# Third hop of a graph layer as seven products, with its weights applied after it

## The chip, the cores and the metric

The kernel runs on one NeuronCore of a Trainium2 chip. Its engines work side by side and meet through semaphores: TensorE (PE, with PEld its weight loads), VectorE (DVE), ScalarE (ACT), GpSimd (POOL) and SyncE (SP), which only starts transfers. The metric is the device time of one execution in microseconds (us), as the median of several runs.

## The reference

Two graph layers on 2048 nodes, 64 features and a batch of 8. Each row of `adj` has equal non-zero entries (one over the row's degree), so a product with it, a hop, is a product with a matrix S of zeros and ones, scaled by row with r.

```python
# layer 0: Chebyshev, K = 3, weights of each node from a 16-wide embedding
w = einsum('nd,dkio->nkio', embedding, weight)       # b in the same way
A_stack = [I, A, 2 A A - I]
x_g = einsum('knm,bmc->bnkc', A_stack, x)
x = layernorm(x + einsum('bnki,nkio->bno', x_g, w) + b)
# layer 1: five matrices from two supports, both adj
x_cat = concat[h, A h, 2 A A h - h, A h, 2 A A h - h]
x = layernorm(h + x_cat @ W + bias)                  # h: output of layer 0
```

With W in five blocks of 64 rows, layer 1 is h v0 + A (h v1 + A (h v2)) + bias, where v0 = I + W0 - W2 - W4, v1 = W1 + W3, v2 = 2 (W2 + W4). Two hops serve each layer: the first and second for x, the third and fourth for h.

## The kernel before

**Tiles.** Nodes are cut into 16 tiles of 128 (index t for results, k for sources). z0, z1 and z2 each hold 16 tiles of 128 x 512 values (batch times features). S is made on the chip from slabs of `adj` by a test against zero (`places`, L196) or against the row's r with a count of the equal places (`places_equal`, L201). A value is split into a high and a low half (`high` on ACT, `low` on DVE), and PE multiplies S with both, so a block costs two matmuls of 512 columns (`add_block`, L229).

**First and second hop.** `hop_x` (L396) runs over k in two passes, counts S's places (`nonzero`, ACT, L445) and writes four sums of quarters of S as bf16 into DRAM (`sums_of`). The second hop, `seven_products` (L460), takes the four quarters of S and the batch in two halves and forms seven products in place of eight blocks, a Strassen scheme: 7 products of 8 steps `kk`, 8 matmuls each (L529), with S as the moving operand, so the result comes out transposed. M1 with B11 needs quarter (0, 0) of S, M6, M7, M5 and M3 load sums, M2 and M4 load quarters. `sum_of_y` makes sums and differences of y on DVE; `put` adds a finished product to the results.

**The mix of layer 0.** `mix0` (L321) goes through 16 node tiles. For each it multiplies x, the first and the second hop, transposed, with all 16 embedding slices of the weights: eight groups of 24 float32 records on PE (L342), each group followed by four multiply-adds on DVE (L348) into `acc`, which POOL has started (L328). Then come `layernorm` (L303: sums on DVE, subtraction on POOL, squares on ACT, a root, and a multiplication on POOL, L312), a transpose of the normalized tile on PE (L268) and `project` (L353): z0 = h v2, z1 = h v1, z2 = h v0 + bias. The transpose of tile t-1 and the operands of tile t+1 are put into tile t by `between`; the projection of t-1 follows tile t.

**Third and fourth hop.** `hop_h` (L599) computes z1 += r S z0 in three passes over k, for 4, 8 and 4 result tiles, with the counting test. `hop_g` (L675) computes z2 += r S z1 for the first 8 result tiles over all k, keeping the halves of z1; `hop_tile` (L697) then does tiles 8 to 15 one by one, in two halves c of 16 matmuls, and normalizes and stores each. `check` (L648), at tile 9, compares the counts; `load_flag` (L660), at tile 10, has each engine read the flag that decides at the end whether a general program runs in addition.

**What sets the order.** A framework plans each engine's queue from a model of times. Where an instruction goes through `ordered` while `in_order` is set, or through `keep_in_program_order`, it is kept behind all that its engine has been given in program order. `run` (L236) takes a list of steps; each has parts with a lead, and a part with lead 2 is written two steps ahead of its use. `todo` holds small pieces of work, two of which are written after each step. PSUM has four tiles of two banks (`bank`, L81), given out in turn; a new tile waits until the last reader of the old one is done. SP's loads stay in program order, with five buffers for raw slabs.

Of the kernel before, what the change touches and what calls it, by code (L numbers as in the profile page):

```python
# [8 lines left out]
F32 = mybir.dt.float32  # L9
# [28 lines left out]
def pattern(  # L38
# [20 lines left out]

    nc = tc.nc  # L60
# [13 lines left out]
    rowpool = pool(hops, "frow", 1, side="right")  # L74
    hpool = pool(hops, "fhl", HL, side="right")
# [23 lines left out]
    equal = keep.tile([P, 3 * NT], F32, tag="equal", name="equal")  # L99
# [13 lines left out]
    v = const.tile([P, 3, C], F32, tag="v", name="v")  # L113
# [122 lines left out]
    def run(steps):  # L236

        got = [{} for _ in steps]
# [23 lines left out]
    def transpose(src, tag, pt=None):  # L262
# [7 lines left out]
        nc.scalar.copy(  # L270
            tt.rearrange("p j (h n) -> p h j n", h=2), pt[:, :, : B // 2 * C].rearrange("p h (j n) -> p h j n", n=C)
        )
# [5 lines left out]
    def rsqrt(ss):  # L278


        def col(name):
            return (work if ss.shape[1] == B else keep).tile(list(ss.shape), F32, tag=f"{name}{ss.shape[1]}", name=name)

        va = col("ln_v")
        nc.vector.scalar_tensor_tensor(va, ss, 1.0 / C, eps.to_broadcast(list(ss.shape)), ALU.mult, ALU.add)
        sd = col("ln_sd")
        nc.scalar.activation(sd, ss, AF.Sqrt, bias=eps, scale=1.0 / C)  # L287
        r0 = col("ln_r0")
        nc.vector.reciprocal(r0, sd)

        q = col("ln_q")
        nc.vector.scalar_tensor_tensor(q, r0, -0.5, r0, ALU.mult, ALU.mult)
        nc.vector.tensor_tensor(q, q, va, ALU.mult)
        r = col("ln_r")
        nc.vector.scalar_tensor_tensor(r, q, 1.5, r0, ALU.add, ALU.mult)
        return r

    def square_sums(src, to):
        sq = work.tile([P, B, C], F32, tag="ln_sq", name="sq")
        nc.scalar.activation(sq, src, AF.Square)  # L300
        nc.vector.tensor_reduce(to, sq, AX.X, ALU.add)

    def layernorm(src):  # L303

        s = work.tile([P, B], F32, tag="ln_s", name="s")
        nc.vector.tensor_reduce(s, src, AX.X, ALU.add)  # L306
        nc.vector.tensor_tensor(s, s, part, ALU.mult)  # L307
        xc = xcpool.tile([P, B, C], F32, tag="ln_xc", name="xc")
        nc.gpsimd.tensor_tensor(xc, src, wide(s), ALU.subtract)  # L309
        ss = work.tile([P, B], F32, tag="ln_ss", name="ss")  # L310
        square_sums(xc, ss)
        nc.gpsimd.tensor_tensor(xc, xc, wide(rsqrt(ss)), ALU.mult)  # L312
        return xc
# [7 lines left out]
    def mix0(t, tt, between):  # L321
# [4 lines left out]
        for g in range(2):  # L326
            part = acc[:, 4 * g : 4 * g + 4, :]
            nc.gpsimd.tensor_tensor(  # L328
# [3 lines left out]
            )  # L332
            for dg in range(D // DG):
                if g == 1 and dg == D // DG - 1:
                    between()
# [10 lines left out]
                for d in range(DG):  # L346
                    dd = dg * DG + d
                    nc.vector.scalar_tensor_tensor(  # L348
                        part, pm[:, :, :, d, :].rearrange("p j i c -> p (j i) c"), emb_sb[:, t, dd : dd + 1], part, ALU.mult, ALU.add
                    )  # L350
        return layernorm(acc)

    def project(t, hT, pus=None):  # L353


        for g in range(2):
            pm = bank("pu") if pus is None else pus[g]
            for i in range(2):
                for j in range(2):
                    q = slice(j * C, (j + 1) * C)  # L360
                    nc.tensor.matmul(  # L361
                        pm[:, j, i * 3 * C : (i + 1) * 3 * C], lhsT=hT[q, 2 * g + i, :], rhs=v[q],
                        start=True, stop=True,
                    )
            got = pm[:, :, : 6 * C].rearrange("p j (i k c) -> p j i k c", i=2, k=3)
            bs = slice(4 * g, 4 * g + 4)
            for s in range(2):
                nc.scalar.copy(bc(s, t)[:, bs, :].rearrange("p (i j) c -> p j i c", j=2), got[:, :, :, 2 - s, :])
            nc.vector.tensor_tensor(
                bc(2, t)[:, bs, :].rearrange("p (i j) c -> p j i c", j=2), got[:, :, :, 0, :],  # L370
                bias1.unsqueeze(1).unsqueeze(1).to_broadcast([P, 2, 2, C]), ALU.add,
            )
# [10 lines left out]
    S1, S2, S4, S3 = range(4)  # L383
    couple = []
# [11 lines left out]
    def hop_x(g, kk, j):  # L396
# [37 lines left out]
        def use(got):  # L434
# [10 lines left out]
            ordered(nc.scalar.activation(seen, s, AF.Copy, accum_out=nonzero[:, i : i + 1]))  # L445
            if last and g == 1:
# [13 lines left out]
    def seven_products(s, to, more):  # L460
# [3 lines left out]
        sums, kept = [], {}  # L464

        def sum_of_y(kk, name):
# [11 lines left out]
            if name == "T2":  # L478
# [4 lines left out]
                return add(y, add(y, quarter(2, 2), quarter(1, 2), ALU.subtract), quarter(1, 1), ALU.add)  # L483
            y = xcpool.tile([P, BC], F32, tag="ln_xc", name="y")
            if name == "T4":
# [573 lines left out]
```

## Time and profile before

| | |
|---|---|
| three runs, us | 838.54, 838.76, 840.05 (median 838.76) |
| profiled execution, us | 839.63 |
| its span, first to last instruction, us | 837.6 |
| mean granted TensorE clock | 0.994 |
| first hop, from 5.9 us | 116.6 |
| second hop, from 122.5 us | 102.8 |
| mix of layer 0, from 225.3 us | 366.7 |
| third hop, from 592.0 us | 119.7 |
| fourth hop, first 8 tiles, from 711.7 us | 58.2 |
| fourth hop, last 8 tiles, from 769.9 us | 58.5 |
| from the last matmul to the end | 9.2 |

Lengths are in us, read from the matmuls' records. A row of a group names line, engine, operation, result and operands, shapes and count, then busy time, mean duration and idle time before it. [...] what a stream of them costs is the spacing of their starts.

### The profile page before, as it was taken

How to read it: one execution, taken by the hardware profiler on the slowest of the kernel's cores; microseconds unless marked ns; L12 is line 12 of the kernel's file. 1: busy time of each engine (PE TensorE's matmuls, PEld its weight loads, DVE VectorE, ACT ScalarE, POOL GpSimd, SP SyncE). 2: the span in 40 equal slices, each digit the busy share in tenths (PEclk: the TensorE clock that was granted, in tenths of full speed). 3: DMA queues.
4: the chain of work that ended last, by engine and by line, in shares of the span. 5: the costliest groups of instructions: out<-in, count | busy, mean ns of one | idle time of the engine just before them, and what ended most of it. 6: DMA issues, size and time to landing. Idle time of an engine off the chain costs nothing.

```text
span 837.6 us, 14392 instructions
## 1 busy us (share of the span) xinstructions
PE 823.5 (98%) x5614; PEld 732.0 (87%) x5614; DVE 607.0 (72%) x1256; ACT 224.6 (27%) x427; POOL 128.8 (15%) x130
## 2 busy tenths in 40 slices
PE   9999999999999999999999999989999999999995
PEld 6888888888888999999999999989888878888884
DVE  6868657757878888888788888897867567534662
ACT  5436445772002111111111111101331132401210
POOL 0100000002731111111111111020101020102133
PEclk9999999999999999999999999999999999999998
DMA  9976775558200000000000000120256227544462
GB/s 332 394 273 221 248 258 174 154 163 289 88 14 14 11 6 13 14 14 13 14 14 13 14 14 14 42 86 2 76 182 190 94 74 240 173 142 126 132 183 92
DMA packets 57180, 96.55 MB, mean 115 GB/s; under 512 B 3984, under 2 KB 28816, under 8 KB 56976
## 3 DMA queue, kind: packets, MB, share of 16 engines
q1 hardware_dynamic: 52208, 82.69, 30.6%
q0 software_dynamic: 2304, 8.39, 3.0%
q10 hardware_dynamic: 2592, 4.47, 1.5%
q8 instruction: 47, 0.77, 0.4%
q14 instruction: 29, 0.24, 0.1%
HBM read 82.94 MB, written 12.58 MB: 114 GB/s over the span
## 4 chain that ended last, share of the span: by engine, by line
PE 93%; DVE 4%; issue 1%; DMA 0%; ACT 0%; POOL 0%; SPq 0%; DVEq 0%; POOLq 0%
PE pm L342 36%; PE acc L229 35%; PE accT L529 12%; PE a L229 7%; DVE acc L348 3%; PE pu L361 2%; PE pt L268 1%; PE first L133 1%; DVE s L205 0%; DMA raw<-in_adj 0%; POOL got L318 0%; DVE s L306 0%; ACT L287 0%; PE accT L144 0%; POOL xc L309 0%
## 5 line engine op out<-in xcount | busy, mean ns | idle before, releaser
L229 PE MATMUL acc<-hl,s 128*128 128x512 f32 x1280 | 292.7, 390 | 0.3 <-DVE acc L348 0.3
L229 PEld LDWEIGHTS acc<-hl,s 128*128 128x128 f32 x1280 | 239.4, 188 | 52.9 <-issue 1.2
L348 DVE SCALAR_TENSOR_TENSOR acc<-pm,pack_sb,acc 128x256 f32<-128x256 f32 x512 | 246.3, 483 | 43.5 <-PE pm L342 21.1
L342 PE MATMUL pm<-w,xt 64*128 64x256 f32 x1024 | 161.1, 379 | 3.1 <-DVE acc L348 2.8
L342 PE MATMUL pm<-w,z 64*128 64x256 f32 x1024 | 160.4, 378 | 0.0
L342 PE MATMUL pm<-w,t 64*128 64x256 f32 x1024 | 160.1, 377 | 0.2 <-ACT t L270 0.2
L342 PEld LDWEIGHTS pm<-w,xt 64*128 64x128 f32 x1024 | 108.1, 188 | 5.6 <-issue 1.8
L342 PEld LDWEIGHTS pm<-w,t 64*128 64x128 f32 x1024 | 110.7, 188 | 2.0 <-ACT t L270 0.6
L342 PEld LDWEIGHTS pm<-w,z 64*128 64x128 f32 x1024 | 110.8, 188 | 1.4
L198 DVE TENSOR_SCALAR s<-raw 128x1024 fp32r<-128x1024 f32 x87 | 68.1, 783 | 57.8 <-PE acc L229 48.8
L529 PE MATMUL accT<-s,hl 128*128 128x512 f32 x448 | 102.0, 389 | 0.0
L529 PEld LDWEIGHTS accT<-s,hl 128*128 128x128 f32 x448 | 84.0, 188 | 17.5
L209 ACT CAST hl<-z 128x512 fp32r<-128x512 f32 (+1 forms) x120 | 67.0, 578 | 119.1 <-PE acc L229 108.5
L213 DVE TENSOR_TENSOR hl<-z,hl 128x512 fp32r<-128x512 f32 (+1 forms) x120 | 81.5, 681 | 13.6 <-ACT hl L209 10.7
L205 DVE SCALAR_TENSOR_TENSOR s<-raw,rrow 128x512 fp32r<-128x512 f32 (+1 forms) x48 | 45.8, 956 | 26.7 <-PE acc L229 25.3
L270 ACT COPY hT<-pt 128x512 f32<-128x512 f32 x16 | 9.4, 586 | 204.4 <-PE pt L268 204.4
L309 POOL TENSOR_TENSOR xc<-acc,s 128x512 f32<-128x512 f32 x16 | 17.1, 1068 | 282.4 <-DVE s L307 282.4
L229 PE MATMUL a<-hl,s 128*128 128x512 f32 x256 | 58.5, 390 | 0.0
L229 PEld LDWEIGHTS a<-hl,s 128*128 128x128 f32 x256 | 48.0, 188 | 10.0
L258 POOL TENSOR_TENSOR z<-z,got 128x512 f32<-128x512 f32 x12 | 18.8, 1592 | 155.2 <-ACT got L257 155.1
L328 POOL TENSOR_TENSOR acc<-z,ebias 128x256 f32<-128x256 f32 x32 | 27.0, 866 | 87.1 <-ACT hl L209 85.6
L517 ACT CAST s<-raw 128x1024 fp32r<-128x1024 bf16 x32 | 33.6, 1050 | 10.6 <-ACT hl L209 10.6
(87 smaller groups left out, 477.0 us busy)
## 6 DMA issues: line engine op xcount, KB each, us to landing
raw<-in_adj SPq DMA_DIRECT2D x103, 512.0 KB, 4.5
raw<-in_adj SPq DMA_DIRECT2D x34, 256.0 KB, 3.0
sums_of<-z POOLq DMA_DIRECT2D x16, 512.0 KB, 4.9
raw<-sums_of SPq DMA_DIRECT2D x32, 256.0 KB, 2.8
xt<-in_xT SPq DMA_DIRECT2D x16, 256.0 KB, 2.7
out<-got ACTq DMA_DIRECT2D x16, 256.0 KB, 2.0
z<-in_x SPq DMA_DIRECT2D x15, 256.0 KB, 9.3
w<-in_w SPq DMA_DIRECT2D x3, 512.0 KB, 5.8
```

Of the source, the lines that this page charges most:

```text
L198: ordered(nc.vector.tensor_scalar(s, raw, 0.0, None, ALU.not_equal))
L205: ordered(nc.vector.scalar_tensor_tensor(s, raw, 0.0, r, ALU.add, ALU.is_equal, accum_out=count))
L209: ordered(nc.scalar.copy(to[0], src))
L213: ordered(nc.vector.tensor_tensor(to[1], src, to[0], ALU.subtract))
L229: nc.tensor.matmul(accs[i], lhsT=s[:, i * P : (i + 1) * P], rhs=hl[h], start=(first and h == 0), stop=(last and h == 1),)
L258: ordered(nc.gpsimd.tensor_tensor(to, to, got, ALU.add))
L309: nc.gpsimd.tensor_tensor(xc, src, wide(s), ALU.subtract)
L328: nc.gpsimd.tensor_tensor(part.rearrange("p (j i) c -> p j i c", j=2), bc(0, t)[:, 4 * g : 4 * g + 4, :].rearrange("p (i j) c -> p j i c", ...
L342: nc.tensor.matmul(pm[:, j, i], lhsT=tt[k][q, 2 * g + i, :], rhs=w[k][q, ds, :], start=(k == 0), stop=(k == 2),)
L348: nc.vector.scalar_tensor_tensor(part, pm[:, :, :, d, :].rearrange("p j i c -> p (j i) c"), emb_sb[:, t, dd : dd + 1], part, ALU.mult, ALU.add
L517: ordered(nc.scalar.copy(s, got["raw"]))
L529: nc.tensor.matmul(acc[i][:, c], lhsT=hl[h][:, i * P : (i + 1) * P], rhs=S[:, c * 512 : (c + 1) * 512], start=(kk == 0 and h == 0), stop=( ...
```

## The change

**Third hop.** z0 now holds h itself. A second call of `seven_products` computes S h, transposed, into four tiles `zT` (float32). `project` multiplies with v0 and v1 only (128 columns instead of 192). The weights v2 are applied to the result: `weigh` multiplies blocks of zT with `v[:, 2]`, and `add_weighed` adds r times that to z1. Half tiles of the first eight are weighed after products M3 and M2, the other eight tiles inside the fourth hop's first part.

**Quarters and sums.** `hop_x` also writes the quarters of S of the second half of the sources to DRAM as bf16, from ACT's queue (`quarters`), and both calls of `seven_products` load them for M2 and M4. T4's sum of y is made in place at product 3. `wait` is the number of empty pieces ahead of a product's puts: 4 in the second hop, 2 in the third.

**Order.** The layernorm of tile t is given out in four parts and kept in order with the projection of t-1. For the last tile the whole mix is kept in order, the first two steps of the third hop are written into it (`early`), and its layernorm's rest goes into `todo`. Its transpose and projection sit in product 0.

**Fourth hop.** The counting test moves there: `hop_g` serves 6 tiles instead of 8 with it, `hop_tile` does tiles 6 to 15 with it. The check comes at tile 14, the flag's matmul and its reading between the halves of tile 15.

**Memory.** rowpool and hpool stay to the end, v moves to `keep`, `equal` and `sums` change their sizes.

```diff
-    v = const.tile([P, 3, C], F32, tag="v", name="v")
+    v = keep.tile([P, 3, C], F32, tag="v", name="v")
-    equal = keep.tile([P, 3 * NT], F32, tag="equal", name="equal")
+    equal = keep.tile([P, 5 * NT], F32, tag="equal", name="equal")
...
     def hop_x(g, kk, j):
...
+            if j == 1:
+                ordered(nc.scalar.dma_start(out=quarters[kk, :, :, g, :], in_=seen))
...
     def layernorm(src, to):
...
-        nc.gpsimd.tensor_tensor(xc, src, wide(s), ALU.subtract)
+        ordered(nc.gpsimd.tensor_tensor(xc, src, wide(s), ALU.subtract))
+        yield
+        sq = squares(xc)
+        yield
...
+        ordered(nc.vector.tensor_reduce(ss, sq, AX.X, ALU.add))
+        root = rsqrt_parts(ss)
+        next(root)
+        yield
+        xc, r = (a.rearrange("p (g m) c -> p g m c", g=2) for a in (xc, wide(next(root))))
+        ordered(nc.gpsimd.tensor_tensor(to, xc, r, ALU.mult))
+        yield
...
     def mix0(t, tt, at):
...
-            nc.gpsimd.tensor_tensor(
+            ordered(nc.gpsimd.tensor_tensor(
                 part.rearrange("p (j i) c -> p j i c", j=2),
...
+                for work_here in at.get((g, dg), ()):
+                    work_here()
...
     def project(t, hT, pus=None):
...
-                        pm[:, j, i * 3 * C : (i + 1) * 3 * C], lhsT=hT[q, 2 * g + i, :], rhs=v[q],
+                        pm[:, j, i * 2 * C : (i + 1) * 2 * C], lhsT=hT[q, 2 * g + i, :], rhs=v[q, 0:2, :],
...
-    def seven_products(s, to, more):
+    def seven_products(s, to, sums, more, wait=4):
...
             def load_sum(got):
-                if isinstance(which, tuple):
+                if which == (0, 0):
                     return
...
+                if isinstance(which, tuple):
+                    load(nc.sync, raw, quarters[kk, :, which[0]])
...
+                if p == 3:
+                    sum_of_y(kk, "T4")
...
+                while p == 6 and todo:
+                    todo.pop(0)()
...
+    def weigh(ts, pairs, bs):
+        for n, t in enumerate(ts):
+            to = columns(pairs, n, bs)
+            for i in range(2 * len(bs)):
+                for j in range(2):
+                    q, block = slice(j * C, (j + 1) * C), 2 * bs[0] + i
+                    nc.tensor.matmul(
+                        to[:, j, i * C : (i + 1) * C], lhsT=zT[t // 8, t // 4 % 2][q, t % 4, block * P : (block + 1) * P],
+                        rhs=v[q, 2, :], start=True, stop=True,
+                    )
+    def add_weighed(ts, n, pairs, bs):
...
+            nc.vector.scalar_tensor_tensor(
+                to, columns(pairs, n, bs), rcol[:, t : t + 1], to, ALU.mult, ALU.add
...
+    third = seven_products(0, to_zT, sums3, {
+        (0, 4): [last_transposed],
+        (0, 6): [last_projected],
+        4: half_weighed(1, 0), 5: half_weighed(0, 1),
+    }, wait=2)
...
+        at = {(1, 3): [between]}
+        if t == NT - 1:
+
+            in_order.append(True)
+            at = {
+                (0, 1): [lambda: early(0)], (0, 3): [lambda: early(1)], (1, 0): [between],
+                (1, 1): [lambda: project(t - 1, done["hT"])],
+            }
+        norm = mix0(t, tt, at)
+        in_order.append(True)
+        next(norm)
+        if t == NT - 1:
+            todo.extend(lambda: next(norm) for _ in range(3))
+            break
...
-    EARLY = 8
+    G = 6
-    sums = keep.tile([P, 8, B], F32, tag="sums", name="sums")
+    sums = keep.tile([P, G, B], F32, tag="sums", name="sums")
...
     def hop_g(k):
...
-            got["s"] = places(slab(k, 0, HALF))
+            got["s"] = places_equal(slab(k, 0, G * P), 0, equal[:, k : k + 1])
...
+            add_block(accs[:4], s, hl, k == 0, end)
+            waiting.append((s[:, 4 * P :], hl, k == 0, end))
+            if k > 0:
+
+                while waiting:
+                    add_block(accs[4:], *waiting.pop(0))
+            if k in (1, 2, 4, 5):
+
+                ts, pairs = {1: [8, 9], 2: [10, 11], 4: [12, 13], 5: [14, 15]}[k], [sums3[0][1]]
+                weigh(ts, pairs, [0, 1])
+                for n in range(2):
+                    add_weighed(ts, n, pairs, [0, 1])
...
     def hop_tile(t, c):
...
-            got["s"] = places(raw)
+            nc.vector.scalar_tensor_tensor(
+                s, raw, 0.0, rrow[:, t * P : (t + 1) * P].unsqueeze(1).to_broadcast([P, 8, P]),
+                ALU.add, ALU.is_equal, accum_out=equal[:, i : i + 1],
+            )
...
+                if t == NT - 1:
+                    make_flag(*late_values["bad"])
+                    late_values["odd"] = load_flag()
                 return
-            if t == 9:
-                check()
-            if t == 10:
-                late_values["odd"] = load_flag()
+            if t == NT - 2:
+                late_values["bad"] = check()
```

## The prediction

> **What bounds the kernel now.** I read the page first: who is busy, and what the chain that ended last consists of.
>
> ```profile
> PE 823.5 (98%) x5614; PEld 732.0 (87%) x5614; DVE 607.0 (72%) x1256; ACT 224.6 (27%) x427; POOL 128.8 (15%) x130
> ...
> PE 93%; DVE 4%; issue 1%; DMA 0%; ACT 0%; POOL 0%; SPq 0%; DVEq 0%; POOLq 0%
> ```
>
> TensorE is the bound nearly everywhere, so a matmul removed is worth its spacing, and the 4% in which DVE carries the chain are places where TensorE was made to wait. Next the busy time by stage (columns: stretch, length, then busy time of PE, PEld, DVE, ACT, POOL, granted clock, DMA share, GB/s): layer 0 mix, third hop, fourth hop's first half, fourth hop's tiles.
>
> ```profile
> 225.30:592.00 366.70, 363.32 (x3561) 356.44 (x3560) 299.86 (x674) 52.83 (x124) 64.62 (x67) 1.00 0.06 18
> 592.00:711.70 119.70, 119.40 (x538) 97.43 (x537) 81.91 (x157) 35.20 (x62) 12.24 (x8) 1.00 0.48 149
> 711.70:769.90 58.20, 58.20 (x257) 47.92 (x256) 24.43 (x37) 10.37 (x19) 4.47 (x3) 1.00 0.52 157
> 769.90:828.40 58.50, 58.50 (x259) 47.87 (x257) 33.60 (x85) 11.94 (x25) 21.05 (x19) 1.00 0.45 138
> ```
>
> Then the chain in order of time (start, length, what), for spacings and for the loss late in the mix.
>
> ```profile
> 130.85 94.52 PE accT L529 x416
> ...
> 338.79 18.13 PE pm L342 x168
> ...
> 563.92 4.52 PE pm L342 x24
> 568.44 1.32 PE pu L361 x16
> 569.76 18.13 PE pm L342 x168
> ```
>
> A 512-column matmul of the hops costs 94.52/416 = 0.227 us. The mix's 256-column records cost 18.13/168 = 0.108 us. Twenty-four of them took 4.52 us at 563.92 instead of 24 x 0.108 = 2.6. The next windows say why: PE idle for half a window, then the clock at half.
>
> ```profile
> 561.50:565.00 3.50, 1.71 (x24) 1.49 (x21) 3.11 (x8) 1.16 (x2) 0.00 (x0) 0.99 0.00 0
> 565.00:568.30 3.30, 3.30 (x20) 3.14 (x18) 0.88 (x2) 0.00 (x0) 0.00 (x0) 0.50 0.00 0
> ```
>
> Tile 14 of the mix lasts 27.5 us from one projection to the next (540.8 to 568.2) where its neighbours take 22.57: 4.9 us are lost, because four slabs of the third hop's tests (L205, from 543.7 to 549.4) were slipped into DVE's queue there.
>
> [...] The node bias (L144, 64 columns, four row groups, two records for each float32 matmul) agrees:
>
> ```profile
> 128.73 1.07 PE L529 MATMUL accT<-s,hl 128*128 128x512 f32 x4
> 129.73 1.12 PE L144 MATMUL accT<-bias_sb 16*128 16x64 f32 x32
> 130.78 0.73 PE L529 MATMUL accT<-s,hl 128*128 128x512 f32 x2
> ```
>
> Its 32 records are 8 rounds of four, and the single records start 112 ns apart from round to round: [...]. The visit cost 1.25 us in all (129.64, when the next L529 was due, to 130.78, plus 0.11 in the slower first pair), so 0.35 us beyond 8 x 0.112 for going in and out. [...] The trace shows it once: 1.71 us busy of 3.5 tripped it, while 2.68 of 3.4 at 264.6 did not. [...]
>
> **The change, part by part**, against the profiled span of 837.6 (its own run took 839.6, 0.9 above the median of 838.76; I carry differences to the median).
>
> 1. Third hop: 7 x 8 steps of 8 matmuls are 448 instead of 512. 64 x 0.227 = **-14.5**.
>
> 2. Projection: 128 columns instead of 192. Its 16 records are 8 rounds in 1.30 us, 0.162 each, by columns. At 128 columns the columns would take 0.108, the weight load 0.112: 8 x 0.112 = 0.90, so -0.40 per tile, 16 tiles: **-6.5**. Two of four ACT copies per tile (375 ns) go too, off the path.
>
> 3. Weights behind the hop: each tile has 8 float32 matmuls of 64 columns with a fresh 128-column load, 16 records, two row groups, 8 rounds x 0.112 = 0.90. 16 tiles are 14.3, in 6 visits (two in the third hop, four in the fourth) at 0.35: **+16.5**. Bounds: were they as quick as the transposes (64 columns, 0.25 us for 8 records), 7.9 + 2.1 = 10; with load and columns one after the other (112 + 54 ns), 21 + 2 = 23. I take 16.5 because part 2's rate and L144's agree on it. So the arithmetic of 1 to 3 is -4.5.
>
> 4. Losses that go with the old order: tile 14 (-4.9), the third hop's first two matmuls, 0.99 us apart where 0.56 was usual (-0.4), and the bank boundary at 687.7 (-0.4). **-5.7**.
>
> 5. The last mix tile in written order. Before, POOL starts tile t+1's accumulator (L328) between the two layernorm multiplications, and DVE may go on as soon as ln_r is done:
>
> ```profile
> 571.79 1.04 POOL L309 TENSOR_TENSOR xc<-acc,s 128x512 f32<-128x512 f32 x1 [19.36 <-DVE s L307]
> 575.60 1.05 POOL L312 TENSOR_TENSOR xc<-xc,ln_r 128x512 f32<-128x512 f32 x1 [2.77 <-DVE ln_r L295]
> ```
>
> Now in tile 15 the start of the accumulator is queued on POOL behind tile 14's final multiplication. Counting from PE's first matmul of tile 15: ln_r is ready at 5.7, the multiplication ends 6.9, the accumulator 7.8 (0.87), DVE's first of eight groups of four (4 x 0.52 = 2.1) starts at 8.0 instead of 5.8. Nothing else stands behind it on POOL, but DVE has nothing it may do first. Into DVE's queue come two early steps of the third hop, each a low half (0.42) and a test (0.69), 1.2 with gaps; their slabs are behind the last xT on SP, issued a tile earlier. DVE ends groups 0 to 3 at 10.1, 13.4, 15.6 and 18.9. PE's four groups (2.59 each) end at 10.4; four PSUM tiles are full, the transpose of tile 14 takes the first freed, so group 4 waits for group 1: 13.5 instead of 10.6. The projection of tile 14 then waits for group 3's tile: 19.0 instead of 16.6. 2.9 + 2.4 = **+5.3**. What is late next is the layernorm of tile 15 by as much.
>
> 6. Start of the third hop. Steps 0 and 1 are ready, so PE runs 3.6 us. Behind the last group DVE has, from PE's last mix matmul: the group until 2.3, the layernorm sums 0.85, two low halves 0.9, the test of step 2 0.7: 4.8, PE wanted it at 3.7. Step 3's operands come after the wait for the squares (5.8) at 7.1, wanted 6.7; for steps 3 to 5 the sums of y (three 0.42) raise DVE's step to 2.45 against PE's 1.82. I add 1.1 + 0.5 + 0.3 + 0.8 = **+2.7**; 0 to 5 as bounds. Later products fit: DVE's fullest (T1 sums, T4 sums, low halves, four puts of 0.68) is 13 of 14.5 us; ACT's (1.05 + 0.40) x 8 is 11.6.
>
> 7. Flag. PE reads it half a tile (16 x 0.227 = 3.6 us) before its end instead of when it had long been there:
>
> ```profile
> L661 PEldq TENSOR_LOAD <-flag x1: 487/487/487, 788.0 to 788.0; - x1
> ```
>
> DVE finishes the previous layernorm 3.6 us after its tile (824.7 against 821.1), so it is free just then. The flag takes 0.13, the load 0.49, three hand-overs and a restart about 0.4: **+1.0** in which the 16 last matmuls are queued behind the load, and for them waits the tail. The other engines' loads are behind finished work; the six early tiles' stores (1.1 us of POOL, 0.35 of ACT) are over by tile 12. Bounds 0.6 and 2.5.
>
> 8. At nothing. The 16 writes of quarters (4.2 MB, ACT's queue, 0.35 us issue each) lie beside hop one, where ACT is half idle and slabs land early from step 4 on (14.4 against 20.8 at PE); without that cover 10 us of transfer would show. Casts for two products move from DVE (0.69) to ACT (1.05), inside the 1.82 us steps. Tests of the fourth hop: DVE per slab 1.04 + 0.08 + 0.75 = 1.9 of PE's 2.7 (768 columns, between the 0.79 and 1.29 of the L205 rows), with four times 1.5 us of adding beside 2.15 us of PE weighing; per tile 6.6 to 8 of 7.28, with two half tiles of lead. Were the lead gone, 1 us per tile for three tiles. Equal addresses: the tiles ahead of S grow by 512 bytes (v 768, `equal` 128, `sums` -64, five columns of its root -320), so S stands to the y halves modulo 256 as before, and I take 0; that PE's spacing would change by 2% either way is the bound I can't exclude (9 us), and nothing points to it. The tail of 9.2 us stays.
>
> Sum: -4.5 - 5.7 + 5.3 + 2.7 + 1.0 = -1.2, without the clock. The new stalls are 2.9, 2.4, then 1.1 + 0.5 and 1.0 us, each in or near a 3.4 us window. A half-clock window costs up to 1.7. The first is hidden by the wait for group 3; of the later three I charge two: +3.4. **+2.2: 841.0.**
>
> **Rivals.** (A) The forecast: seven products pay for their weights, and ordering gives back what it saved: 838.5 to 843.5, 0.55, of it 0.37 slower by over 0.2% (1.7 us, about what a measurement tells from no change) and 0.18 the same. (B) Faster: the written order costs half of parts 5 and 6 and no further half-clock window follows: -1.2 - 4.0 = 833.5; it decides once DVE reaches tile 15's first group by 6 us or PE's stalls stay under 2.5 us. For it: DVE's idle time at each tile's end; against it: the queue as written. 0.27, of it 0.23 faster. (C) DVE becomes the bound: in the first product, where it runs at 2.45 against 1.82 us, and in the fourth hop's tests and additions, 5 us more: 846. For it DVE's 82 of 120 us in the third hop already; against it the light products after the fifth. 0.18, of it 0.14 slower, 0.04 the same. (D) That seven products aren't shorter can't be: the second hop shows 448 at the same spacing.
>
> Faster 0.23, same 0.26, slower 0.51; likeliest A with 841.0. Leaving out a tenth on either side gives 834 to 846; A's own range is 838.5 to 843.5.
>
> **What would show it.** 448 third-hop matmuls at 0.227; projections of 0.90; weighing records 56 ns apart on average, 3.6 us for the visits of 8 half tiles; no loss in tile 14; waits of PE for L348 in tile 15 near 11 and 17 us after its start; half clock once or more between there and the second product; a PE gap of about 1 us half a tile from the end. Wrong if the weighing is loaded at the transposes' rate (-6), if tile 15 runs without a gap, or if stalls appear from the second product on.

## The result, and the profile after

The changed kernel took 839.98 us (median of 20 runs, 838.72 to 842.57), the kernel before 839.27 beside it: a ratio of 1.0012 (95% interval 1.0005 to 1.0019). Seven products instead of eight blocks, narrower projections and a repaired order come out about even. The profiled execution of the changed kernel took 839.43 us, its span 837.4, against 839.63 and 837.6; the two had mean clocks of 0.997 and 0.994, to which the part on the clock returns.

The page of the changed kernel, busy times and chain by engine:

```profile
PE 819.1 (98%) x5806; PEld 727.0 (87%) x5806; DVE 595.3 (71%) x1295; ACT 267.4 (32%) x464; POOL 111.9 (13%) x121
...
PE 84%; DVE 6%; DMA 5%; issue 2%; ACT 1%; POOL 1%; SPq 0%; ACTq 0%; DVEq 0%; POOLq 0%
```

TensorE has 4.4 us less work than before (823.5), and the chain leaves it more often: DMA carries 5% of it where it carried none, DVE 6% instead of 4%. The stages (first hop, mix, third hop, then the fourth hop's two parts; columns as before):

```profile
5.99:123.50 117.51, 117.28 (x514) 96.28 (x513) 87.68 (x139) 58.24 (x105) 8.93 (x16) 1.00 0.93 327
...
226.50:588.00 361.50, 356.75 (x3561) 348.79 (x3560) 292.66 (x665) 44.73 (x97) 60.90 (x66) 1.00 0.07 21
588.00:701.90 113.90, 112.15 (x603) 92.37 (x602) 69.71 (x162) 73.75 (x116) 2.16 (x2) 1.00 0.43 142
701.90:754.00 52.10, 52.10 (x321) 43.14 (x320) 33.42 (x61) 5.55 (x9) 0.00 (x0) 1.00 0.46 141
754.00:827.70 73.70, 72.93 (x323) 59.88 (x321) 46.98 (x118) 13.14 (x28) 24.81 (x18) 1.00 0.46 147
```

| stage, by the starts of TensorE's records, us | before | after | difference |
|---|---|---|---|
| first hop | 116.5 | 117.55 | +1.0 |
| second hop | 102.9 | 102.9 | 0 |
| mix | 366.7 | 361.6 | -5.1 |
| third hop | 119.7 | 113.8 | -5.9 |
| fourth hop, to the last matmul | 116.4 | 125.6 | +9.3 |
| from the last matmul's start | 9.5 | 9.9 | +0.4 |

The mix and the third hop give 11 us, the weighing (8.6 us) and the flag (0.8) in the fourth hop take most of it, and the first hop takes one. Below, "the changed kernel" is the profile above; times of other kernels are given as ratios to the kernel before, run beside them.

### The profile page after: what moved, and what is told of

It reads as the page before. It is cut to its first block, busy times and chain, and to the rows that moved or that the text cites. A ratio compares the mean times of both kernels' runs of the same rounds, so it can differ in the third digit from the quotient of the medians.

```text
span 837.4 us, 14780 instructions
## 1 busy us (share of the span) xinstructions
PE 819.1 (98%) x5806; PEld 727.0 (87%) x5806; DVE 595.3 (71%) x1295; ACT 267.4 (32%) x464; POOL 111.9 (13%) x121
## 4 chain that ended last, share of the span: by engine, by line
PE 84%; DVE 6%; DMA 5%; issue 2%; ACT 1%; POOL 1%; SPq 0%; ACTq 0%; DVEq 0%; POOLq 0%
PE pm L362 36%; PE accT L561 24%; PE a L231 8%; PE acc L231 7%; PE accT L231 5%; DMA quarters<-seen 4%; DVE acc L368 3%; PE accT L671 2%; PE pu L381 1%; DMA raw<-in_adj 1%; PE pt L274 1%; DMA z<-in_x 1%; DVE s L200 1%; DVE z L416 1%; ACT seen L468 1%
## 5 line engine op out<-in xcount | busy, mean ns | idle before, releaser
L561 PE MATMUL accT<-s,hl 128*128 128x512 f32 x896 | 205.6, 390 | 1.7 <-DVE s L200 1.7
L561 PEld LDWEIGHTS accT<-s,hl 128*128 128x128 f32 x896 | 167.5, 188 | 37.8 <-ACT sq L310 1.8
L231 PE MATMUL acc<-hl,s 128*128 128x512 f32 x512 | 117.5, 391 | 0.2 <-DVE z L453 0.2
L549 ACT CAST s<-raw 128x1024 fp32r<-128x1024 bf16 x96 | 100.8, 1050 | 44.3 <-ACT hl L211 32.4
L231 PEld LDWEIGHTS acc<-hl,s 128*128 128x128 f32 x512 | 96.1, 188 | 21.5 <-DVE z L453 1.4
L211 ACT CAST hl<-z 128x256 fp32r<-128x256 f32 (+1 forms) x96 | 47.5, 510 | 62.5 <-PE acc L231 27.7
L231 PE MATMUL accT<-hl,s 128*128 128x512 f32 x192 | 44.9, 392 | 0.0
L231 PEld LDWEIGHTS accT<-hl,s 128*128 128x128 f32 x192 | 35.7, 188 | 7.6
L200 DVE TENSOR_SCALAR s<-raw 128x1024 fp32r<-128x1024 f32 x47 | 33.2, 706 | 11.8 <-PE acc L231 8.0
L468 ACT ACTIVATE seen<-s 128x1024 bf16<-128x1024 f32 x32 | 33.7, 1053 | 17.9 <-DMA quarters<-seen 17.9
```

The costliest lines, as they stand in the source:

```text
L200: ordered(nc.vector.tensor_scalar(s, raw, 0.0, None, ALU.not_equal))
L211: ordered(nc.scalar.copy(to[0], src))
L231: nc.tensor.matmul(accs[i], lhsT=s[:, i * P : (i + 1) * P], rhs=hl[h], start=(first and h == 0), stop=(last and h == 1),)
L549: ordered(nc.scalar.copy(s, got["raw"]))
L561: nc.tensor.matmul(acc[i][:, c], lhsT=hl[h][:, i * P : (i + 1) * P], rhs=S[:, c * 512 : (c + 1) * 512], start=(kk == 0 and h == 0), stop=( ...
```

## The experiments

### The flag's place

```diff
                 if t == NT - 1:
                     make_flag(*late_values["bad"])
-                    late_values["odd"] = load_flag()
                 return
+            if t == NT - 1:
+                late_values["odd"] = load_flag()
```

> After the change TensorE stands still for 0.96 us half a tile from its end, while DVE makes the flag and TensorE reads it. Here the flag is made at the same place, but read only behind the last 16 matmuls. Theory (the 16 matmuls queue behind the reading): the gap falls to the 0.3 us that the flag's own small matmul costs, so about 0.65 us less than the changed kernel's 839.98, that is 839.3. Rival (the reading only moves into the tail, where DVE, ACT or POOL now read it while the last tile waits): the gap goes, the stretch after the last matmul grows by 0.5 us, and the time stays at 840.0.

Measured: 839.41 us, 1.0000 (0.9992 to 1.0008): 0.6 less than the changed kernel by the medians, 1.0 by the ratios, whose intervals overlap, so that the trace is the firmer evidence. TensorE's timeline, first of the changed kernel, then of this one (start, length, what; in brackets idle time before it and what ended it):

```profile
823.01 0.19 PE L763 MATMUL pf<-ones,bad 128*1 128x1 f32 x2
823.96 3.91 PE L231 MATMUL a<-hl,s 128*128 128x512 f32 x16 [0.77 <-DVE flag L764]
```

```profile
823.96 0.19 PE L763 MATMUL pf<-ones,bad 128*1 128x1 f32 x2
824.08 3.94 PE L231 MATMUL a<-hl,s 128*128 128x512 f32 x16
```

From the flag's matmul to the next takes 0.12 us instead of 0.96, and the stretch from the last matmul's start grows by 0.1 only (9.95 to 10.04), against the rival. The queue behind the reading was the cost: 0.84 us, more than the 0.65 of the theory.

### POOL's start set free, and the place of the early steps

The first kernel takes the start of the accumulator out of the written order; the second does that too and moves the two early steps.

```diff
-            ordered(nc.gpsimd.tensor_tensor(part..., bc(0, t)..., ebias..., ALU.add))
+            nc.gpsimd.tensor_tensor(part..., bc(0, t)..., ebias..., ALU.add)
```
```diff
-                (0, 1): [lambda: early(0)], (0, 3): [lambda: early(1)], (1, 0): [between],
-                (1, 1): [lambda: project(t - 1, done["hT"])],
+                (1, 0): [between], (1, 1): [lambda: project(t - 1, done["hT"])],
+                (1, 2): [lambda: early(0)], (1, 3): [lambda: early(1)],
```

> One edit to the changed kernel: in the last mix tile POOL's start of the accumulator is not kept behind tile 14's final multiplication. Theory (step 5: DVE's first group waits for this start): DVE begins about 2.2 us earlier, TensorE's two waits in tile 15 (2.49 and 1.39 us) shrink to under 1.5 us together, and the time falls by 2.0 to 2.5 us to about 837.7. Rival (DVE's own work in tile 15, the two early steps of 1.2 us each, sets the waits): they stay above 3 us together, and the time stays within 0.5 us of 840.0.

> As the kernel with POOL's start set free, and the two early steps of the third hop put before the last two groups of tile 15 instead of the second and the fourth. Theory (DVE is short in the whole of tile 15 and the third hop's start, where it is idle for under 1.5 us): the wait at tile 14's projection (2.27 us there for 0.89 of work) goes, and the start of the third hop, 11.68 us for its first 40 matmuls, loses as much; the time stays within 0.5 us of 838.97. Rival (only the place of the two steps made TensorE wait): both together fall by 1.4 us, and the time to 837.5.

Measured: 838.97 us, 1.0000 (0.9991 to 1.0009), and 837.76, 0.9986 (0.9980 to 0.9993). TensorE's waits in tile 15 and at the third hop's start, in the changed kernel:

```profile
575.12 0.70 PE L362 MATMUL pm<-w,xt 64*128 64x256 f32 x4 [2.30 <-DVE acc L368]
...
580.06 0.70 PE L362 MATMUL pm<-w,xt 64*128 64x256 f32 x4 [1.19 <-DVE acc L368]
...
593.38 3.88 PE L561 MATMUL accT<-s,hl 128*128 128x512 f32 x16 [1.39 <-DVE s L200]
```

With POOL's start free:

```profile
574.20 0.70 PE L362 MATMUL pm<-w,xt 64*128 64x256 f32 x4 [0.34 <-DVE acc L368]
...
579.14 0.70 PE L362 MATMUL pm<-w,xt 64*128 64x256 f32 x4 [1.19 <-DVE acc L368]
```

And with the early steps later:

```profile
577.79 0.70 PE L362 MATMUL pm<-w,xt 64*128 64x256 f32 x4 [0.27 <-DVE acc L368]
...
591.72 7.29 PE L561 MATMUL accT<-s,hl 128*128 128x512 f32 x24 [2.02 <-DVE s L200]
```

The first wait was POOL's: 2.30 became 0.34, the 2 us that were expected; the median shows 1.0 less than the changed kernel, half of what was expected, and the section on the first hop tells what hides the rest in this profile. The second doesn't move with it, and goes when the early steps do. I had expected the third hop's start to take that gain back. In this profile it does: the first 40 matmuls took 13.18 us instead of 11.68. But the longer wait of 2.02 was followed by half clock (0.53 granted from 593 to 596 us), and eight matmuls that started 0.43 apart instead of 0.23 account for the whole 1.5 us; the stalls themselves are nearly as long in sum (2.02 against 1.43 and 0.39). The median is 1.2 us under that with POOL's start alone, so the rival fits better: the place of the steps made TensorE wait, DVE was not short over the whole stretch. The intervals of the two kernels still touch.

### Weights in the projection, transposes behind the hop

```diff
-                        pm[:, j, i * 2 * C : (i + 1) * 2 * C], ..., rhs=v[q, 0:2, :],
+                        pm[:, j, i * 3 * C : (i + 1) * 3 * C], ..., rhs=v[q],
...
+            ordered(nc.scalar.copy(z0_part, got[:, :, :, 2, :]))
...
-                    nc.tensor.matmul(
-                        to[:, j, i * C : (i + 1) * C], lhsT=zT[...], rhs=v[q, 2, :], start=True, stop=True)
+                    nc.tensor.transpose(to[:, j, i * C : (i + 1) * C], zT[...], ident[q, q])
```

> The changed kernel with seven products, but the weights v2 put back into the projection (192 columns) and the product's blocks only transposed by TensorE, not multiplied, where they were weighed. Theory (a visit costs what its float32 multiplications take at 56 ns a record, two records each, and a transpose is one record at 31 ns or so, 0.25 us for 8 in the mix): the visits of 3.72 us fall to about 1.4 and those of 1.93 to 0.8, together -9; the 16 projections go from 0.89 to 1.30 us, +6.5, of which up to 2.5 come out of the 0.19 us that TensorE now waits for DVE in each mix tile; net -3 to -5: 835 to 837. Rival (loading 128 columns of weights at 112 ns sets the pace of transposes too): visits of 2.1 and 1.2 us, -6.2, net 0 to -2: 838 to 840.

Measured: 833.13 us, 0.9933 (0.9919 to 0.9947), more than the theory's -5. The records of the weighing in the changed kernel and of the transposes here (minimum, median and maximum in ns, first and last start, shapes):

```profile
L671 PEld LDWEIGHTS accT<-v,zT x256: 182/188/188, 670.5 to 726.4; 64*128 64x128 f32 x128
L671 PE MATMUL accT<-v,zT x256: 272/272/320, 670.5 to 726.5; 64*128 64x64 f32 x128
```

```profile
L673 PEld LDWEIGHTS accT<-ident,zT x128: 135/139/142, 674.3 to 720.0; 64*128 64x128 f32 x128
L673 PE MATMUL accT<-ident,zT x128: 221/223/272, 674.3 to 720.1; 64*128 64x64 f32 x128
```

Half as many records, and the rounds of two start 62 ns apart instead of 112. A visit is a stretch of such records between the hop's matmuls, timed here from its first record to the hop's next. Visits take 1.15 us instead of 3.72 (two) and 0.64 instead of 1.93 (four): -10.3 in all. The mix takes 364.8 us instead of 361.6: of 15 x 0.41 = 6.2 us that narrower projections save, 3.0 had been given back, so their return costs 3.2 only. With 0.4 for the projection in the third hop that is -6.7; the two profiled executions differ by 6.64.

### Half of the weights' columns

```diff
-                        to[:, j, i * C : (i + 1) * C], lhsT=zT[...],
-                        rhs=v[q, 2, :], start=True, stop=True,
+                        to[:, j, i * C : i * C + C // 2], lhsT=zT[...],
+                        rhs=v[q, 2, : C // 2], start=True, stop=True,
```

> The changed kernel with 32 of the 64 weights' columns left out in the multiplications behind the third hop, so half of each block of weighed values is not computed. Theory (part 3: a round of two records costs its 128-column weight load, 0.112 us, whatever the columns): the visits stay at 3.72 and 1.93 us, the time at 840. Rival (64 float32 columns set the pace, and the load is as quick as for the transposes, whose rounds took 62 ns): rounds of about 62 ns, visits of 2.1 and 1.1 us, and 6.5 us less, 833.5.

Measured: visits of 3.69 and 1.90 us, where the clock is full. Halving the columns takes 1 to 2% off, so the columns don't set the pace here. That the load of the stationary operand sets it, as the theory said, was not shown: a fixed price of such a record would look the same. The time rose to 843.55, 1.0043 (1.0026 to 1.0060), for another reason: the mean clock of the profiled execution was 0.989. Of its 5.6 us over the changed kernel's span, 2.5 lie in the first hop, which this edit doesn't touch (see the copies of S), and 3.1 in the third: half clock from 694.84 us on, still in the second visit, stretched the next 40 matmuls from 9.20 to 12.00 us. The two windows there (columns as before; the third number from the end is the granted clock):

```profile
691.43:694.84 3.41, 3.41 (x60) 3.23 (x58) 1.21 (x4) 1.04 (x1) 0.00 (x0) 1.00 0.80 217
694.84:698.25 3.41, 3.41 (x16) 2.86 (x15) 2.11 (x6) 0.00 (x0) 0.00 (x0) 0.50 0.19 71
```

The first is filled with the visit's records, of 32 columns each, for 3.23 us, and TensorE counts as busy throughout; yet the clock was halved. In five profiles whose records have all 64 columns such a window (they are counted in the part on the clock) holds 3.11 to 3.29 us of a visit, and full clock followed each time. In this execution half clock cost more than the missing columns saved; that they brought it about is not shown by one execution.

### The first hop's copies of S

```diff
-            seen = work.tile([P, 2, Q], BF16, tag="ln_sq", name="seen")
+            seen = work.tile([P, 2, Q], BF16, tag="ln_sq" if j == 1 else "acc", name="seen")
```

> The changed kernel, with the bf16 copies of S in the first hop in two pairs of buffers: those that are written to memory as quarters in one pair, the others in another. Theory (ACT stands in its queue until a quarter's transfer has left the one pair of buffers, falls behind by 5 us, and then hands over the first pass's results late, for which TensorE waits): the 4.0 to 5.3 and 4.17 us of the two steps at the end of the first pass go back to 3.63 to 3.7, the first hop from 117.6 to 118.8 us to about 116.5, the time by 1 to 2 us to 838 to 839. Rival (the transfers themselves hold back the slabs of the second pass): the first hop keeps its 117.6 or more, and the time stays at 840.

Measured: 838.54 us, 0.9992 (0.9984 to 1.0000), less than the changed kernel by 1.4 (medians) to 1.7 us (ratios). ACT's waits in the changed kernel's first hop (total, times, longest), then the end of the chain up to the first pass's end:

```profile
ACT seen L468 <- DMA quarters<-seen: 17.9, 5, 5.4
```

```profile
49.99 6.87 DMA quarters<-seen
...
64.25 0.67 DVE z L453
...
64.97 58.73 PE acc L231 x256
```

And the chain with the copies apart:

```profile
6.55 116.45 PE acc L231 x512
```

A copy that is written out occupies one of two buffers until its transfer has landed, up to 8.4 us after issue, while a step takes 3.63. ACT gets late, the first pass's results are handed over late in its queue and in DVE's, and TensorE waits for PSUM. With the copies apart, the wait is gone and the chain is TensorE alone. In the changed kernel the two steps there took 4.01 and 4.17 us; in the kernel with POOL's start free 5.30 and 4.17. So the price is 0.9 us in one execution and 2.2 in another, which also hides part of that kernel's gain. In the kernel with half of the weights' columns half clock followed the same wait, and the two steps took 5.61 and 5.45, 3.8 us too many. The spread of the times fits this: 13 executions with the copies apart lie between 838.21 and 838.89 us, the 20 of the changed kernel between 838.72 and 842.57.

### The order of the kernel before

```diff
     behind = ExitStack()
+    in_order.append(True)
     run(third + ...
```

> The kernel before, with one edit: the third hop's tests and low halves are kept behind the mix in DVE's queue, so that no slab's test comes between tile 14's multiply-adds. Theory (the loss of 4.9 us in tile 14 is of the old order and needs no third hop of seven products to go): tile 14 takes 22.6 us, the start of the third hop loses up to 2 us because tests and halves come later, and the time falls from 839.27 by 3 to 5 us, to 834.5 to 836.5. Rival (the four tests of 0.69 to 1.3 us and their halves only move to the start of the third hop, where TensorE then waits for them): within 1 us of 839.3.

Measured: 840.10 us, 1.0010 (1.0003 to 1.0017). Tile 14 takes 22.57 us now, and the third hop starts late. TensorE's timeline there:

```profile
590.55 13.69 PE L229 MATMUL acc<-hl,s 128*128 128x512 f32 x52 [3.79 <-ACT sq L300]
```

After this idle time come 3.4 us at half clock (591.7 to 595.1). The loss moved with the tests, and the rival holds: the 4.9 us in tile 14 were the price of a prompt start, and not free to take.

### Addresses

Both kernels shorten the tile of counts by columns that nothing uses, to 48 columns (128 bytes less, shown here) or to 64 (64 bytes less). That shifts S, and leaves the halves of y in the first three hops where they are.

```diff
-    equal = keep.tile([P, 5 * NT], F32, tag="equal", name="equal")
+    equal = keep.tile([P, 3 * NT], F32, tag="equal", name="equal")
```

> The changed kernel with 128 bytes less in the tile of counts (its unused columns), so that S in the first three hops no longer stands at the same address modulo 256 as the halves that it is multiplied with (96 against 224). Theory (addresses cost nothing, step 8): the spacing of the hops' matmuls stays 0.227 us, the third hop 113.8 us, the time 840.0 within 0.7. Rival (equal addresses are what keeps the spacing): the spacing grows by 1% or more in the first three hops, 3 us in all, 843 or more.

> The changed kernel with 64 bytes less in the tile of counts, so that S stands at 160 modulo 256 and the halves of the first three hops at 224. Theory (only equality modulo 256 is quick, every other distance costs the same): spacing of 0.234 us in the second hop as at a distance of 128, and about 847.9. Rival (the cost grows with the distance): spacing between 0.227 and 0.234, and 842 to 846.

Measured: 847.86 us, 1.0104 (1.0088 to 1.0120), and 847.13, 1.0093 (1.0078 to 1.0109). My theory fell in the first. The chain through the second hop, in the changed kernel, at 128 bytes and at 64:

```profile
132.01 94.52 PE accT L561 x416
```

```profile
133.95 97.26 PE accT L561 x416
```

```profile
133.82 97.26 PE accT L561 x416
```

The spacing is 0.234 us instead of 0.227, for 64 bytes as for 128, and the time is near the theory's 847.9. But this doesn't hold for every hop. In the first, where S is the stationary operand and not the moving one, the starts are 0.232 apart for 128 bytes and 0.229 for 64: there 128 bytes cost more than 64, as the rival said. In the fourth hop only half of the tiles' y is apart: with 128 bytes, half tiles whose y stands at 224 beside S at 96 have starts 0.2328 apart, those with both at 96 0.2276, in turn through all tiles, where the changed kernel has 0.2267; with 64 bytes it is 0.2301 and 0.2282. That ties it to the two operands' addresses, and not to a shift of everything else. That the distance counts modulo 256 is my assumption: in the changed kernel, as in the one before, the operands of every hop stand a multiple of 512 bytes apart, and no run has them 256 apart.

### All together, and casts in the first product

The first kernel joins the edits on the flag, POOL's start, the copies and the transposes. The second adds this (`of_x` is true in the second hop only, and the third hop's step loads from `corner` and casts); the third moves the early steps as well.

```diff
+            else:
+                ordered(nc.scalar.dma_start(out=corner[kk, :, g, :], in_=seen[:, 0]))
...
-                if which == (0, 0):
+                if which == (0, 0) and of_x:
                     got["s"] = places(slab(kk, 0, HALF))
```

> What the single edits gave, in one kernel: weights in the projection and transposes behind the third hop, POOL's start set free, the copies of S apart, the flag read behind the last matmuls. Theory (the places are apart in time, so the gains add): 833.13 - 0.6 - 1.9 - 1.5 = 829 (828 to 830.5). Rival (DVE, which has more to do around tile 15 than TensorE, takes back what POOL's start gives, and the clock dips elsewhere): 831 to 833.

> As the kernel with all single edits together, and the first product of the third hop gets its quarter of S as bf16 too, written in the first hop and cast by ACT, where DVE tested a slab of adj (0.69 us a step). Theory (steps 5 and 6: DVE's work sets TensorE's waits in tile 15 and in the first product): the wait at tile 14's projection falls from 1.4 us to 0.7, the first 40 matmuls of the third hop from 11.67 us to about 10, the time from 828.86 by 2 to 3 us to 826 or 827. Rival (ACT's queue takes over: its casts of 1.05 us stand behind the wait for the last layernorm's squares): the first 40 matmuls take 11.7 us or more, and the time stays within 1 us of 828.9.

> The kernel with casts in the first product, and its two early steps before the last two groups of tile 15. Theory (DVE has room once the tests are gone, so the later place no longer costs at the third hop's start what it gives in tile 15): TensorE waits under 0.5 us at tile 14's projection, and the time is 0.5 to 1.5 us under that with casts alone, about 826. Rival (the two low halves or ACT's casts are then late for the hop's first steps): no gain, or up to 1 us more than with casts alone.

Measured: 828.86 us, 0.9880 (0.9864 to 0.9896); 826.90, 0.9856 (0.9841 to 0.9871); 826.71, 0.9852 (0.9839 to 0.9866). The gains add up: 829 was expected of the first. TensorE's waits in the first of the three, then with casts:

```profile
580.10 0.70 PE L362 MATMUL pm<-w,xt 64*128 64x256 f32 x4 [0.78 <-DVE acc L368]
...
593.43 3.95 PE L563 MATMUL accT<-s,hl 128*128 128x512 f32 x16 [1.43 <-DVE s L200]
```

```profile
593.81 3.92 PE L568 MATMUL accT<-s,hl 128*128 128x512 f32 x16 [1.60 <-ACT s L556]
```

With DVE's tests gone, the wait in tile 15 is gone (1.2 us from the transpose to the hop) and the first 40 matmuls take 11.18 us instead of 11.67; what is left there waits for a cast of ACT, so theory and rival both have a part (about 10 us, or 11.7 and more, were expected). With the tests gone, the early steps' place no longer matters: the intervals of the last two kernels overlap, and the 0.5 to 1.5 us that the theory of the last one expected didn't come.

## Why the prediction was right, and where it was not

The forecast was 841.0 us, 2.2 above the median that it started from, with "slower" likeliest (0.51). Measured were 0.7 more by the medians and 0.12% (0.05 to 0.19) by the ratio: inside its range, and less than the 0.2% that the forecast took as the border of "slower". That the total is so near is in part luck. The sum without the clock was -1.2 and the profiled executions differ by -0.2, but inside it errors of 3 us and more cancel: the clock was charged with 3.4 that this profile doesn't show, and step 2 was credited with 3.0 that weren't on the path.

| step | forecast | measured |
|---|---|---|
| 1 third hop, 64 matmuls fewer | -14.5 | -14.5 |
| 2 projection | -6.5 | -6.5, then +3.0 given back |
| 3 weights behind the hop | +16.5 | +16.5 |
| 4 losses of the old order | -5.7 | gone; not free (see its experiment) |
| 5 last mix tile | +5.3 | +3.9 |
| 6 start of the third hop | +2.7 | +2.5 |
| 7 flag | +1.0 | +0.84 |
| 8 quarters, tests, addresses | 0 | +1.0, first hop |
| clock | +3.4 | 0 in this execution |

With -5.7 for step 4 the measured column makes about +1.0. The 1.2 us down to -0.2 are not accounted for one by one; half of it are two tiles of the mix of the kernel before that took 22.85 and 22.90 us and that step 4 doesn't list.

**Step 2 left out who frees the bank.** The rate was right, 0.89 us per projection. But it forgot that tile by tile TensorE ran close to DVE. The chain shows the group after the transposes take 2.85 us where 2.65 was usual, first before and then after the change:

```profile
334.84 2.65 PE pm L342 x24
```

```profile
538.97 0.89 PE pu L381 x16
...
558.49 2.85 PE pm L362 x24
```

TensorE, 0.41 us sooner, waits about 0.19 for DVE to free a PSUM tile, and the period goes from 22.57 to 22.36. With the columns back the wait is gone, the period is 22.57 again, and they cost 3.2 and not 6.2: half of this step's gain was never on the path.

**Step 3** held. The rounds are as priced: 3.72 us for 64 records and 1.93 for 32 make 0.056 a record and 0.14 for the visit. The hop's matmuls just ahead of a visit and behind it are slower by 0.23 in sum, so a visit costs 0.37 beside its records, where 0.35 was taken from the node bias's (1.05 from first record to next matmul, 1.27 in all). Two of 3.95 and four of 2.16 make 16.5. The pace came from the node bias, 112 ns a round, and with half of the moving columns the rounds stay near it (visits of 3.69 us instead of 3.72). That this is the price of loading 128 stationary columns was my estimate and is not shown: the transposes, with the same 64 x 128 block as stationary operand, have rounds of 62. The lower bound of 10 us, "as quick as the transposes", priced multiplications; with transposes in their place the six visits cost 6.3, counted in the same way. This alternative was the largest gain at hand.

**Step 4** was read from one execution, and 1.9 of the 4.9 us in tile 14 are its half clock (4.52 us for 24 matmuls instead of 2.6). In the batch run beside the first experiments, 13 of 41 executions of the kernel before have that profile's mean clock of 0.994, with a median of 839.97; the 28 with 0.996 and more have 838.69. So most of them seem to lose less in tile 14 than the profile, and the median had less to gain than the profile showed. No trace of such an execution was kept.

**Step 5** named both waits and their causes: 2.9 and 2.4 forecast, 2.49 and 1.39 measured, from start to start less the usual. The first went with POOL's start, the second with the early steps. That an engine works in the order of its queue, on which both rest, was my assumption; it fits these two runs (2.30 us became 0.34, and 1.19 became 0.27). Only the place of the second is off by one: tile 14's projection started at once, and the group behind it waited. **Step 6** is right in size; the experiment with casts shows DVE's tests to be 0.5 us of it, and ACT's queue, which the step did not count, the next in line. **Step 7** held: in the changed kernel the flag took 0.15 us and TensorE's reading of it 0.49, which leaves 0.20 of the 0.84 for the hand-overs and the restart, where 0.4 was my estimate.

**Step 8 failed for the quarters.** "ACT is half idle" is an average: it is idle because it waits, and with two buffers and transfers of up to 8.4 us it waits for what it has itself sent. The cover that the step named was for slabs; the price lay in buffers. **For the addresses** the 0 is right because the change leaves S and y where they stood to each other, and the bound of 9 us that I could not exclude is what a shift costs: 7 to 8 us. The tests in the fourth hop are free, as said: its tiles show 0.2267 throughout.

**The clock charge failed.** Within one trace the clock changes whole multiples of 3.413 us apart: in the kernel before it falls to half at 564.955 us, is full again at 568.368 and falls at 831.195, so the changes are 1 and 77 times that length apart. Windows can thus be counted from a change; where they lie differs from trace to trace (in the changed kernel the clock falls at 832.72). Here are the window with the first wait of tile 15 in the changed kernel, then the one in the kernel with S shifted by 64 bytes and its next:

```profile
573.31:576.72 3.41, 1.60 (x15) 1.64 (x17) 3.09 (x8) 0.19 (x1) 0.00 (x0) 1.00 0.49 154
```

```profile
576.94:580.35 3.41, 1.12 (x18) 1.01 (x16) 3.16 (x7) 0.59 (x1) 0.00 (x0) 1.00 0.51 149
580.35:583.76 3.41, 3.41 (x20) 3.25 (x18) 3.27 (x8) 0.00 (x0) 0.00 (x0) 0.50 0.08 14
```

Of all windows counted so in the 14 profiles, those with idle time that were followed by half clock have TensorE busy, by its records, for 1.62 us or less of 3.41, and those followed by full clock for 1.57 or more. An estimate from these numbers: where half clock followed, about 1.8 us of the window or more had been idle (3.41 less 1.62). The stalls that were charged (1.19, then 1.39 and 0.36, then 0.77 at the flag) are each shorter, and the windows with them had 2.02 us busy or more in the changed kernel. Only tile 15's first wait leaves a window as little busy as those; of seven profiles with it two show half clock there (mean clocks of 0.994 and 0.989, the kernels with 64 bytes and with half of the columns). As the prediction had said, it is hidden there: the second wait is gone, and from the transpose to the third hop it takes 15.86 us in both, 15.65 in the changed kernel.

What the clock did in the changed kernel's other executions is known only as a mean: 8 of 20 have 0.996 or 0.997, as the profile has, and a median of 839.55 us; 12 have 0.994 or 0.995, and 840.58. All nine profiles without half clock between start and end have at least 0.996, the five with it at most 0.995. So half clock seems to have come in many of them, and the wait for the copies in the first hop is a likely place, but no trace shows it. A profile with a dip before the change and one without after it would also explain why the profiles differ by -0.2 and the medians by +0.7.

**The rivals.** B asked for half of steps 5 and 6 and no dip: there was no dip in this profile, but 6.4 of 8.0 us were there. C, DVE as the bound of the first product and of the fourth hop with 5 us more, did not happen: in the first product it cost what step 6 had counted, in the fourth hop nothing.

## What to carry to other kernels

Before pricing a faster TensorE step, ask who frees the PSUM tile that follows it: here half of the saving went to a wait of 0.19 us per tile. When an engine sends a transfer from a buffer that it fills itself, compare buffers times step with the transfer's time to landing (here 2 x 3.63 us against up to 8.4), not with the engine's busy share. Where a layout has to be changed behind a matmul and a weight can be applied ahead of it, try transposes behind in place of multiplications: here they cost 6.3 us against 16.5, for 3.6 in the projections.

## What the runs showed of the hardware that I had not expected

- In the changed kernel, whose hops have the moving and the stationary operand a multiple of 512 bytes apart, float32r matmuls of 512 columns start 0.227 us apart. With S shifted by 64 or 128 bytes they start 0.234 us apart in both cases where S moves (second hop); where it is stationary, 0.229 and 0.232 (first hop), 0.230 and 0.233 (fourth hop's tiles). Other distances weren't tried. Inside the fourth hop's tiles equal halves come to 0.2276 and 0.2282 in the shifted kernels and not to 0.2267; why stays open.
- For the same stationary block of 64 x 128 float32, the load records of the transposes have a median of 139 ns and those of the multiplications 188, with rounds of 62 against 112 ns.
- In the 14 profiles, cut into windows of 3.413 us from a change of the clock on, those with idle time and half clock after them were busy for 1.62 us or less, and those with full clock after them for 1.57 or more, so near 1.6 both were seen. The same wait of 2.3 us led to either.
- A window that TensorE spent on float32 matmuls of 64 rows and 32 columns (3.23 us of 3.41), busy by its records throughout, was followed by half clock, seen once; with 64 columns (3.11 to 3.29 us) full clock followed in five profiles.
